# A GRU followed by a mixture of experts: the projections' bias added by VectorE as deferred work, zero copies and row deals moved to other steps

## The chip, the cores and the metric

The kernel runs on one core of a Trainium2 chip. Its time is the device time of one execution in microseconds (us). The kernel before was run three times: 1398.75, 1398.89 and 1401.8 us, median 1398.89 us. The engines are called PE (TensorE, matmuls; PEld is its weight load), DVE (VectorE), ACT (ScalarE), POOL (GpSimd) and SP (SyncE, which here only issues DMAs).

## What is computed

The reference runs a GRU over the time axis of `x` (8 sequences, 256 steps, 512 features) from the initial state `cond`, feeds its states to a mixture of experts (8 experts, the best 2 of each token, and a shared expert), and adds the result to `x`:

```python
def cell(h, x):
    gi = x @ W_ih + b_ih
    gh = h @ W_hh + b_hh
    i_r, i_z, i_n = jnp.split(gi, 3, axis=-1)
    h_r, h_z, h_n = jnp.split(gh, 3, axis=-1)
    r = jax.nn.sigmoid(i_r + h_r)
    z = jax.nn.sigmoid(i_z + h_z)
    n = jnp.tanh(i_n + r * h_n)
    h_new = (1.0 - z) * n + z * h
    return (h_new, h_new)
...
combine = jnp.sum(topk_w[..., None] * jax.nn.one_hot(topk_ids, E, dtype=x.dtype), axis=1)
gu = jnp.einsum('th,ehf->etf', x, w_gate_up)
eo = jnp.einsum('eti,eih->eth', _silu_and_mul(gu), w_down)
routed = jnp.einsum('te,eth->th', combine, eo)
shared = _silu_and_mul(x @ w_sh_gate_up) @ w_sh_down
return (routed + shared).reshape(orig_shape)
```

All arithmetic is float32. The 256 GRU steps are sequential; the input projections `x @ W_ih + b_ih`, the routing and the shared expert are not.

## The kernel before

**Blocks and steps.** The 256 steps are 16 blocks `k` of 16 steps `t`. `step(n)` issues the recurrent matmuls into the PSUM banks `ps_rn` and `ps_z` (L514), and then the chain that makes the next state: DVE transposes r, n and z (L527), ACT does the sigmoids and the tanh (L531, L537, L539) and opens the gates of the next step by copying the projections ("seeds") into PSUM (L486), DVE does the arithmetic (L534, L535, L542, L544) and writes the new state `hT` (L545). The next step's matmuls read `hT`. POOL copies one column of `hn` in every step (L543), so that POOL's later work starts only behind that point of the chain.

**Order.** The order on every engine is the order in which the program issues: `manual_schedule` leaves it as written. One engine's instruction that waits holds up all that were issued behind it on the same engine. SP issues nearly all DMAs and is tied to the steps only by what its DMAs wait for.

**What fills PE.** While the chain of step `n` runs, PE works on a queue of pieces (`matmul_piece`, `Piece`), 8 units of work in each step; a unit is four matmuls over 128 columns. The pieces are the input projections (`project(k, g)`, k the block, g = 0, 1, 2 for r, z, n; 4 pieces of 4 units each, L338) and, from block 2 on, the shared expert (`shared_unit`). They are issued behind `step(n)`, so on PE they stand between the matmuls of step `n` and those of step `n + 1`.

**A projection's end.** When the last piece of `project(k, g)` is issued, `end()` (for k > 0) has ACT copy the PSUM bank to the buffer `gi` (L432), POOL add the bias there (L433), and, after g = 1 and after g = 2, SP send `gi` to DRAM: `gid_rz` (512 KB, the r and z parts of `gi`, L441) and `gid_n` (256 KB, L443). There is one buffer `gi`; each g has its own third of it. Later, `load_seeds` (L475) reads the values back, four steps at a time.

**Deferred work.** `afterward(cost, work)` puts DVE work into one first-in, first-out list with a declared cost in us: the transpose of `x` for a projection (`turn_x_afterwards`, cost 1.1, L327), the product of the shared expert's halves (0.9, L769 and L770) and the final sum (0.66, L862). In each step, behind the chain, `catch_up(room)` takes work from the head of the list while the head's cost fits in what is left of `WINDOW = 1.1` (L350); DVE work that a step does directly (routing, `send_rows`) is taken off that room first. A piece that needs deferred work which has not been issued yet calls its `needed()`, which issues the list up to and including that item on the spot (for `x`: `turned_x.pop(k)()`, L412).

**Rows and zeros.** For the experts, every token's state is dealt into `dealt` in DRAM by an indirect DMA on POOL (`deal_rows`, L681), two per block. Before that, SP copies zeros there (`dealt<-blank`, 256 KB, L1029), eight copies in each block. A deal and a zero copy wait for the landing of the ones issued before them. The weights of the experts and of the shared expert are loaded by POOL's DMAs (`loads`, L166): one per step in blocks 0, 1 and 15, one in every odd step in the others, until the list is empty.

Of the kernel before, what the change touches and what calls it, by code (L numbers as in the profile page):

```python
# [13 lines left out]
ALU = mybir.AluOpType  # L14
# [11 lines left out]
def kernel(  # L26
# [52 lines left out]
    nc = tc.nc  # L79
    B, T, D = x.shape  # L80
    G3 = w_ih.shape[1]
    E = w_gate.shape[1]
# [9 lines left out]
    NM = NTOK // P  # L92
# [98 lines left out]
    def load_expert(e):  # L191
        load_up(e)
        load_down(e)
# [49 lines left out]
    def counting(name, n, base, step, channel):  # L243
# [31 lines left out]
    gi_later = const.tile([P, 4, 3, P], F32, name="gi")  # L275
# [3 lines left out]
        for i in (1, 0)  # L279
    ]  # L280
    gi_dram = [
        [
            dram.tile([4, B, TS, P], F32, name=f"gid_n_{i}"),
            dram.tile([4, B, TS, 2 * P], F32, name=f"gid_rz_{i}"),
        ]
        for i in range(1, NB)
    ]
# [13 lines left out]
    dealt = dram.tile([E * NM + 1, P, D], F32, name="dealt")  # L301
# [8 lines left out]
    blank = dram.tile([P, D], F32, name="blank")  # L310
# [23 lines left out]
    def multiply(ps, lhs, rhs, start, stop):  # L334


        for c in range(4):
            nc.tensor.matmul(  # L338
                ps[32 * c : 32 * c + 32],
                lhs(c),  # L340
                rhs,
                start=start,
                stop=stop,
                skip_group_check=True,
            )
# [29 lines left out]
    def matmul_piece(issue, end=None):  # L375
        return Piece(issue, end)

    def afterward(cost, work):
        item = [cost, work]
        afterwards.append(item)  # L380

        def needed():
            while item in afterwards:
                afterwards.popleft()[1]()

        return needed
# [3 lines left out]
    def bank_of(shape, name):  # L390
        if len(held) == 3:
            for needed in held[0]:
                needed()
        readers = []
        held.append(readers)
        return ps_mm.tile(shape, F32, tag="mm", name=name), readers
# [8 lines left out]
    def project(k, g):  # L405

        box = {}

        def issue(q, cols):
            if q == 0 and cols.start == 0:  # L410
                if k in turned_x:
                    turned_x.pop(k)()  # L412
                box["ps"], _ = bank_of([P, D], f"gip_{k}_{g}")
            multiply(
                box["ps"][:, cols],
                lambda c: xT_of[k][:, c, q, :],
                wih[:, q, g * D + cols.start : g * D + cols.stop],
                start=(q == 0 and cols.start == 0),
                stop=(q == NQ - 1 and cols.stop == D),
            )  # L420

        def by_group(t_):
            return t_.rearrange("p (q j i) -> p j q i", q=NQ, j=4)

        def end():
            gi = gi_later if k else gi_first
            to_gi = gi[:, :, g, :].rearrange("p j (q i) -> p j q i", q=NQ)
            bias_g = by_group(bias[:, g * D : (g + 1) * D])
            if k == 0:
                nc.vector.tensor_tensor(to_gi, by_group(box["ps"]), bias_g, ALU.add)  # L430
            else:
                nc.scalar.copy(to_gi, by_group(box["ps"]))  # L432
                nc.gpsimd.tensor_tensor(to_gi, to_gi, bias_g, ALU.add)  # L433
            if g > 0:
                projected.add((k, "rzn"[g]))
            if g > 0 and k == 0:
                send_first(g, 0)
            elif g > 0:
                to = gi_dram[k][g % 2].rearrange("j b t n -> (b t) j n")
                if g == 1:  # L440
                    nc.sync.dma_start(to.rearrange("p j (a n) -> p j a n", a=2), gi[:, :, 0:2, :])  # L441
                else:
                    nc.sync.dma_start(to, gi[:, :, 2, :])  # L443

        return [
            matmul_piece(lambda cols, q=q: issue(q, cols), end if q == NQ - 1 else None)
            for q in range(NQ)
        ]

    projected = set()  # L450

    def send_first(g, c):

        rows_ = slice(SC * B * c, SC * B * (c + 1))
        to = gi_first_dram[g % 2][c].rearrange("j t b n -> (t b) j n")
        if g == 1:
            nc.scalar.dma_start(to.rearrange("p j (a n) -> p j a n", a=2), gi_first[rows_, :, 0:2, :])
        else:
            nc.scalar.dma_start(to, gi_first[rows_, :, 2, :])
# [153 lines left out]
    def weigh_all(k):  # L613

        ch, w2 = chosen[k], weight_of[k]
        comb = said_0[:, :, 1]
        nc.vector.tensor_scalar(comb, ch[:, 0, :], w2[:, 0:1], None, ALU.mult)
        nc.vector.scalar_tensor_tensor(comb, ch[:, 1, :], w2[:, 1:2], comb, ALU.mult, ALU.add)
        nc.vector.tensor_scalar(
            said_0[:, :, 0], row_of.broadcast_to([P, E]), 0.0, None, ALU.add  # L620
        )
# [58 lines left out]
    def deal(tile_, at):  # L680
        nc.gpsimd.indirect_dma_start(  # L681
            out=dealt.rearrange("r p d -> (r p) d"),
            out_offset=bass.IndirectOffsetOnAxis(ap=at, axis=0),
            in_=tile_,
            in_offset=None,
        )

    def deal_rows(k, i):
        deal(rows_of[k], rows_at[k][:, i : i + 1])
# [116 lines left out]
    def load_again(k):  # L806

        again[k] = two.tile([P, D], F32, tag="again", name=f"again_{k}")
        nc.sync.dma_start(again[k], x[:, k * TS : (k + 1) * TS, :])
# [196 lines left out]
    for k in range(NB):  # L1006


        at = {}

        def when(t, cost, busy, work):
            at.setdefault(t, []).append((cost, busy, work))

        if k > 0:
            steps_ = (
                (0, choose, 1, 0), (1, sum_logits, 0.5, 0), (2, order_experts, 0, 1.2), (4, weigh, 0, 1.0),
                (5, count_places, 0.5, 0), (6, give_places, 0, 1.2), (8, send_rows, 0, 0.75), (10, read_rows, 0, 0),
            )
            late = int(k == 1)
            for t, f, cost, busy in steps_:  # L1020
                when(t + late, cost, busy, lambda f=f, k=k: f(k - 1))
            if k == 1:
                when(6, 0, 0.7, lambda k=k: weigh_all(k - 1))
            for i in range(2 if k > 1 else E):
                to_enter.append((k * TS + 8 + 2 * i, lambda k=k, i=i: enter(k - 1, i)))
            for i in range(2):
                when(12 + late + 2 * i, 0, 0, lambda k=k, i=i: deal_rows(k - 1, i))
        for e in range(E):
            when(2 + e, 0, 0, lambda k=k, e=e: nc.sync.dma_start(dealt[e * NM + k], blank))  # L1029
        if k > 1 and k % 2:  # L1030
            for b in (3, 2):
                when(6, 0, 0, lambda k=k, b=b: load_again(k - b))
        if k == 2:
            for e in range(3):
                load_expert(e)
            load_up(3)
        if k == NB - 1:
            load_down(3)
            for e in (E - 2, E - 1):
                load_expert(e)  # L1040
        quota = 33 * NQ if k < 2 else sum(p.left() for p in projections) / max(1, NB - 1 - k)
        while projections and quota > 0:
            quota -= projections[0].left()
            queue.append(projections.popleft())
        assert k == NB - 1 or len(projections) <= 13 * (NB - 2 - k), "the next block's are made"
        if k > 1:
            half = NSH * NF // 2
            for u in range(half):
                feed_shared(k // 2 - 1, half * (k % 2) + u)
        for t in range(TS):  # L1050
            n = k * TS + t
            step(n)
            if (n + 1) % SC == 0 and n + 1 < T and (n + 1) // SC + NS - 1 < T // SC:
                load_seeds((n + 1) // SC + NS - 1)
            room = WINDOW
            for cost, busy, work in at.get(t, ()):
                work()
                spent += cost
                room -= busy
            if to_enter and to_enter[0][0] == n:  # L1060
                to_enter.popleft()[1]()
            catch_up(room)
            if loads and (k < 2 or k == NB - 1 or t % 2):
                loads.popleft()()

            due += PER_STEP
            while queue and (queue[0].left() == 0 or due - spent >= queue[0].cost):
                spent += queue[0].run(due - spent)
                if queue[0].left() == 0:
                    queue.popleft()  # L1070
            if not queue:
                spent = due
# [4 lines left out]
    k = NB - 1  # L1077
# [77 lines left out]
```

## Time and profile before

| | |
|---|---|
| runs shown, median | 1398.89 us (1398.75 to 1401.8) |
| profiled execution's own time | 1401.84 us |
| its span, first to last instruction | 1400.0 us |
| mean granted PE clock | 0.996 |
| the 256 steps (first to last `hT`) | 37.28 to about 1148 us |
| PE busy, 33 to 1150 us | 1110.43 of 1117 us |
| DVE / ACT / POOL busy, 33 to 1150 us | 552.78 / 441.38 / 208.21 us |
| the bias on POOL (L433) | 45 instructions of 1274 ns |

A line of the timeline has its start, its duration, the engine, the source line, the operation, output and inputs by the program's names, and the count of instructions merged into it; in square brackets the idle time before it and what ended that. In a row of instruction groups, the part behind the first bar is busy time and mean ns of one, and behind the second bar the idle time before them. PE's matmuls are pipelined, and their ends are modelled.

The step is the distance between two starts of L545. Over the 255 distances it is 4.29 to 4.39 us, but for 21 of over 4.40 us, among them 5.68 us (step 14 to 15 of block 1), 5.24 us (step 0 to 1 of block 2), 5.04 and 4.83 us.

### The profile page before, as it was taken

Reading aid. Unit: us, or ns where it says so; the run is one execution under the profiler, and the core shown is the slowest. Engines: PE = TensorE matmul, PEld = TensorE weight load, DVE = VectorE, ACT = ScalarE, POOL = GpSimd, SP = SyncE. Lnnn points to the kernel's source line nnn. Section 1 sums busy time; section 2 is a strip of 40 time slices with the busy share of each in tenths; the row PEclk is TensorE's granted clock in tenths of the full one; section 3 lists DMA queues with packets and bytes.
Section 4 is the critical chain, followed back from the end, with each engine's and each line's share of the span. In section 5 each row is a group of like instructions: output and inputs, shape, how many; then the busy total and the mean of one; then the engine's idle time right before and its main releaser. Section 6 shows DMA issues by size and latency. Waiting matters only on the chain. (4 is left out here: it accounts for less than half of the span.)

```text
span 1400.0 us, 58934 instructions
## 1 busy us (share of the span) xinstructions
PE 1370.8 (98%) x24512; PEld 790.5 (56%) x24512; DVE 655.0 (47%) x2701; ACT 474.7 (34%) x2037; POOL 291.5 (21%) x564
## 2 busy tenths in 40 slices
PE   8999999999999999999999999999999999999996
PEld 3455657665656565656665666566655664444442
DVE  2445444545454544455544554555454543344442
ACT  0444343334343434343434343434343330111110
POOL 3333332121111111111111111111111122133332
PEclk9999999999999999999999999999999999999998
DMA  8544574332332232223222322232223454455553
GB/s 269 171 136 143 123 123 104 111 106 89 101 101 65 76 82 74 67 81 82 82 74 59 82 88 76 66 82 74 67 75 88 121 130 132 92 100 97 101 95 45
DMA packets 94082, 137.62 MB, mean 98 GB/s; under 512 B 17256, under 2 KB 67864, under 8 KB 91768
## 3 DMA queue, kind: packets, MB, share of 16 engines
q1 hardware_dynamic: 77192, 95.54, 24.9%
q0 software_dynamic: 15152, 37.38, 12.3%
q8 instruction: 194, 3.18, 1.0%
q10 hardware_dynamic: 1472, 0.93, 0.3%
q14 instruction: 72, 0.59, 0.1%
HBM read 94.55 MB, written 72.78 MB: 120 GB/s over the span
## 5 line engine op out<-in xcount | busy, mean ns | idle before, releaser
L514 PE MATMUL ps_rn<-we,hT 128*8 128x256 f32 x8192 | 492.1, 379 | 7.5 <-DVE hT L545 3.2
L514 PEld LDWEIGHTS ps_rn<-we,hT 128*8 128x8 f32 x8192 | 226.5, 89 | 254.1 <-ACT ps_z L486 52.0
L527 DVE STREAM_TRANSPOSE rT<-ps_rn 128x128 f32<-128x128 f32 x256 | 81.2, 317 | 436.8 <-PE ps_rn L514 436.8
L514 PE MATMUL ps_z<-we,hT 128*8 128x128 f32 x8192 | 274.3, 273 | 0.4 <-issue 0.4
L514 PEld LDWEIGHTS ps_z<-we,hT 128*8 128x8 f32 x8192 | 229.4, 90 | 50.0 <-issue 1.0
L531 ACT ACTIVATE rT<-rT 128x32 f32<-128x32 f32 x256 | 58.8, 230 | 527.8 <-DVE rT L527 517.8
L543 POOL COPY last_hn<-hn 128x1 f32<-128x1 f32 x256 | 47.3, 185 | 828.5 <-DVE hn L542 825.9
L824 PE MATMUL gu_s<-hc,wsu 128*32 128x256 f32 x3072 | 189.8, 379 | 0.0
L338 PE MATMUL gip<-we,xT 128*32 128x512 f32 (+2 forms) x1872 | 186.0, 520 | 1.7 <-DVE xT L220 1.7
L824 PEld LDWEIGHTS gu_s<-hc,wsu 128*32 128x32 f32 x3072 | 104.2, 110 | 56.5 <-issue 12.6
L778 PE MATMUL gu_t<-we,xrT 128*128 x280 | 131.4, 593 | 1.8 <-issue 1.8
L338 PE MATMUL po<-wsd,act_s 128*32 128x512 f32 (+2 forms) x1272 | 131.2, 509 | 0.2 <-DVE again L862 0.2
L338 PEld LDWEIGHTS gip<-we,xT 128*32 128x32 f32 x1872 | 61.0, 111 | 70.2 <-issue 59.9
L778 PEld LDWEIGHTS gu_t<-we,xrT 128*128 128x128 f32 x280 | 50.5, 190 | 52.9 <-issue 45.2
L527 DVE STREAM_TRANSPOSE zT<-ps_z 128x128 f32<-128x128 f32 x256 | 79.1, 309 | 0.3 <-PE ps_z L514 0.3
L548 ACT COPY hc<-hT 128x32 f32<-128x32 f32 x192 | 47.6, 248 | 91.2 <-DVE hT L545 88.9
L486 ACT COPY ps_rn<-seeds_n 128x128 f32<-128x128 f32 x256 | 69.1, 270 | 8.3 <-DMA seeds_n<-gid_n_first 0.2
L534 DVE TENSOR_TENSOR rT<-nT,rT 128x32 f32<-128x32 f32 x256 | 51.2, 200 | 42.8 <-ACT rT L531 42.2
L527 DVE STREAM_TRANSPOSE nT<-ps_rn 128x128 f32<-128x128 f32 x256 | 70.2, 274 | 0.0
L486 ACT COPY ps_rn<-seeds 128x128 f32<-128x128 f32 x256 | 69.0, 269 | 2.5 <-DMA seeds<-gid_rz_first 1.6
L542 DVE TENSOR_TENSOR hn<-hT,rT 128x32 f32<-128x32 f32 x256 | 49.3, 193 | 38.7 <-ACT rT L537 11.1
L433 POOL TENSOR_TENSOR gi<-gi,bias 128x512 f32<-128x512 f32 x45 | 57.3, 1274 | 46.0 <-ACT gi L432 45.4
(167 smaller groups left out, 1160.3 us busy)
## 6 DMA issues: line engine op xcount, KB each, us to landing
dealt<-blank SPq DMA_DIRECT2D x128, 256.0 KB
xr<-dealt SPq DMA_DIRECT2D x140, 64.0 KB
we<-in_L_ffn_w_gate_up_dram POOLq DMA_DIRECT2D x32, 256.0 KB, 6.8
gid_rz<-gi SPq DMA_DIRECT2D x15, 512.0 KB
seeds<-gid_rz SPq DMA_DIRECT2D x240, 32.0 KB
wsu<-_L_ffn_w_sh_gate_up_dram POOLq DMA_DIRECT2D x16, 256.0 KB, 5.6
rows<-hr SPq DMA_DIRECT2D x128, 32.0 KB
rb<-rows SPq DMA_DIRECT2D x16, 256.0 KB
```

Of the source, the lines that this page charges most:

```text
L338: nc.tensor.matmul(ps[32 * c : 32 * c + 32], lhs(c), rhs, start=start, stop=stop, skip_group_check=True,)
L433: nc.gpsimd.tensor_tensor(to_gi, to_gi, bias_g, ALU.add)
L486: nc.scalar.copy(gate_of[g], src)
L514: nc.tensor.matmul(banks[g][32 * j : 32 * j + B, 0 : n_ * P].rearrange("b (a k i) -> b a k i", a=n_, k=NQ), hT[:, q, 0:B], whh_v[:, q, j, ...
L527: nc.vector.transpose(gT.rearrange("p a b -> p (a b)"), gate_of[g])
L531: nc.scalar.activation(r, r, AF.Sigmoid)
L534: nc.vector.tensor_tensor(r, nT[:, :, 0:B], r, ALU.mult)
L542: nc.vector.tensor_tensor(hn, hT[:, :, 0:B], nn, ALU.subtract)
L543: nc.gpsimd.tensor_copy(last_hn, hn[:, 0, 0:1])
L548: nc.scalar.copy(hc_of_block(k).rearrange("p g q (c t) -> p q g c t", t=TS)[:, :, :, :, t], new.rearrange("p q (g c) -> p q g c", c=2),)
L778: nc.tensor.matmul(box["ps"], lhs(q), w_up(q), start=(q == 0), stop=(q == NQ - 1))
L824: nc.tensor.matmul(box["ps"][32 * g : 32 * g + 32, two_i, :], wsu[c][:, q, two_i, fs], hc_of[m][:, :, q, :], start=(two_i == 0 and q == 0) ...
```

## The change

The bias of the projections k > 0 is added by DVE. ACT's copy to `gi` stays where it was, in `end()`; the add becomes deferred work of cost 0.66, and the send to DRAM is issued behind the add. The first-in, first-out list is the one that holds the other deferred work. Before a third of `gi` is overwritten, its earlier add is issued if it was still in the list.

The deals of rows move from steps 12 and 14 (13 and 15 in block 1) to steps 13 and 15 in all blocks. The zero copies move from steps 2 to 9 to steps 0, 1, 2, 4, 6, 8, 10 and 12; in block 0 all are two steps later.

```diff
             if k == 0:
                 nc.vector.tensor_tensor(to_gi, by_group(box["ps"]), bias_g, ALU.add)
+                if g > 0:
+                    projected.add((k, "rzn"[g]))
+                    send_first(g, 0)
+                return
+            if g in biased:
+                biased.pop(g)()
+            nc.scalar.copy(to_gi, by_group(box["ps"]))
+            biased[g] = afterward(0.66, lambda: add_bias(to_gi, bias_g))
+
+        def add_bias(to_gi, bias_g):
+            nc.vector.tensor_tensor(to_gi, to_gi, bias_g, ALU.add)
+            if g == 0:
+                return
+            projected.add((k, "rzn"[g]))
+            to = gi_dram[k][g % 2].rearrange("j b t n -> (b t) j n")
+            if g == 1:
+                nc.sync.dma_start(to.rearrange("p j (a n) -> p j a n", a=2), gi_later[:, :, 0:2, :])
             else:
-                nc.scalar.copy(to_gi, by_group(box["ps"]))
-                nc.gpsimd.tensor_tensor(to_gi, to_gi, bias_g, ALU.add)
...
+                nc.sync.dma_start(to, gi_later[:, :, 2, :])
...
+    biased = {}
...
-                when(12 + late + 2 * i, 0, 0, lambda k=k, i=i: deal_rows(k - 1, i))
-        for e in range(E):
-            when(2 + e, 0, 0, lambda k=k, e=e: nc.sync.dma_start(dealt[e * NM + k], blank))
+                when(13 + 2 * i, 0, 0, lambda k=k, i=i: deal_rows(k - 1, i))
+        for e, t in enumerate((0, 1, 2, 4, 6, 8, 10, 12)):
+            when(t + 2 * (k == 0), 0, 0, lambda k=k, e=e: nc.sync.dma_start(dealt[e * NM + k], blank))
```

## The prediction, made before the result was known

> **What bounds the kernel now.** I read the page first: PE is busy for 1370.8 of 1400.0 us, and the groups give the price of what is moved (behind the bars: busy us and mean ns, then idle us before them).
>
> ```profile
> L534 DVE TENSOR_TENSOR rT<-nT,rT 128x32 f32<-128x32 f32 x256 | 51.2, 200 | 42.8 <-ACT rT L531 42.2 <-ACT ps_rn L486 0.5 <-issue 0.2
> ...
> L535 DVE TENSOR_TENSOR rT<-nT,rT 128x32 f32<-128x32 f32 x256 | 49.2, 192 | 8.8
> ...
> L433 POOL TENSOR_TENSOR gi<-gi,bias 128x512 f32<-128x512 f32 x45 | 57.3, 1274 | 46.0 <-ACT gi L432 45.4 <-issue 0.5
> ```
>
> Then the timeline of one step in the middle, PE's lines and DVE's:
>
> ```profile
> 608.24 1.91 PE L338 MATMUL gip<-we,xT 128*32 128x512 f32 x16
> 609.96 1.91 PE L514 MATMUL ps_rn<-we,hT 128*8 128x256 f32 x32
> ...
> 609.62 0.19 DVE L545 TENSOR_TENSOR hT<-rT,zT 128x32 f32<-128x32 f32 x1
> 609.73 1.14 DVE L327 STREAM_TRANSPOSE xT<-x 128x512 f32<-128x512 f32 x1
> 611.93 0.32 DVE L527 STREAM_TRANSPOSE rT<-ps_rn 128x128 f32<-128x128 f32 x1 [1.06 <-PE ps_rn L514]
> ```
>
> Call T the start of `hT` (609.62). The next recurrent matmuls start at T+0.34, the next chain at T+2.31 on DVE and at T+2.73 on ACT. PE's fill of 8 units ran from 608.24 to 609.96, 1.72 us or 0.215 us a unit: it ends just when `hT` is there. So chain and fill are level, and anything that holds either lengthens the step. DVE is free from T+0.19 to T+2.31, 2.1 us; ACT copies to `gi` at T+0.35 (609.97, 0.58 us) and is free until T+2.73 (L531 at 612.35). POOL's add follows that copy (610.64 to 611.92) and is over before the chain starts.
>
> **What the GpSimd add costs.** Next, the longest step, 5.68 us, in DVE's and POOL's timeline:
>
> ```profile
> 170.30 1.53 DVE L534 TENSOR_TENSOR rT<-nT,rT 128x32 f32<-128x32 f32 x1 [0.16 <-issue]
> ...
> 170.49 1.28 POOL L433 TENSOR_TENSOR gi<-gi,bias 128x512 f32<-128x512 f32 x1
> 171.70 0.19 POOL L543 COPY last_hn<-hn 128x1 f32<-128x1 f32 x1
> ```
>
> DVE's L534 lasts until POOL's add is over. L535 has the same shape and count and never meets the add; L534's surplus over it is 51.2 - 49.2 = 2.0 us, 1.3 of it here. The change removes these: **-2.0 us** (at least 1.3). The other 43 adds cost nothing on POOL: its work is off the chain, and L542 never waited for L543.
>
> **The add on DVE.** 45 adds at 0.69 us (L430, block 0's add of the same size, 685 ns), 31 us in the free 2.1 us behind the chain. I counted the deferred list by the rules of `catch_up`: no step gets more than 1.86 us of such work, which leaves 0.25. The ACT copy that an add needs ends over 3 us earlier. Cost on DVE: 0. Without the cover an add would cost 0.69 in its step. But the add queues in the same list as the transposes, and delays them. At all but two places the transpose is still a step or more ahead of the projection that reads it. The two are:
>
> **First: step 1 of block 0.** Before:
>
> ```profile
> 37.59 1.18 DVE L327 STREAM_TRANSPOSE xT<-x 128x512 f32<-128x512 f32 x1
> ...
> 40.22 1.91 PE L338 MATMUL gip<-we,xT 128*32 128x512 f32 x16
> ...
> 41.58 0.19 DVE L545 TENSOR_TENSOR hT<-rT,zT 128x32 f32<-128x32 f32 x1
> ...
> 41.94 1.92 PE L514 MATMUL ps_rn<-we,hT 128*8 128x256 f32 x32
> ```
>
> x_2 is transposed behind step 0, and step 1's fill (40.22) reads it. After the change the list before step 0 is: add (1,0) at 0.66, transpose of x_2 at 1.1, add (1,1) at 0.66. Step 0 takes the first (0.44 is left), step 1 the transpose, step 2 the second add. So the transpose stands on DVE behind `hT` of step 1, and PE's fill of step 1, which stands on PE before the matmuls of step 2, waits for it. With T = 41.58: transpose T+0.11 to T+1.26, PE on at T+1.42 (0.16 behind its release, as from L545's end to the matmuls), 8 units of 0.215 to T+3.14, where step 2's matmuls stood at T+0.34: **+2.8 us**, 2.6 to 3.0.
>
> **Second: step 9 of block 1.** The list holds add (5,0), x_6, add (5,1). Direct work of 1.0, 0.7 and 1.2 leaves steps 5, 6 and 7 too little room; step 8 does the add (before: the transpose of x_6). Step 9 has `send_rows`, 0.75, and nothing fits; but `project(6,0)` begins in its fill with 6 units and forces x_6 out on the spot, behind `hr`. From T of step 9: `hr` T+0.11 to T+0.82 (L668, 0.71), x_6 to T+2.0, PE T+2.16, 6 units to T+3.45 instead of T+0.34: **+3.1 us**, 2.8 to 3.3.
>
> **The send, and ACT's next copy into `gi`.** `gid_rz` leaves only after add (k,1), 1 to 3 steps later than before (the first at 31.94 before), and the copy (k+1,0) overwrites what it reads, so ACT waits for its landing, and the chain's sigmoid stands behind that copy. By the count, copy and send are at least 1.8 steps apart except twice. No wait shows a send's landing; the DMA windows around one that starts in a quiet stretch (825.86, with a zero copy behind) bound it:
>
> ```profile
> 827.00:827.50 0.50, 0.50 (x16) 0.25 (x12) 0.50 (x2) 0.25 (x1) 0.00 (x0) 1.00 0.98 352
> 827.50:828.00 0.50, 0.50 (x16) 0.23 (x8) 0.50 (x1) 0.00 (x0) 0.00 (x0) 1.00 0.97 338
> 828.00:828.50 0.50, 0.50 (x16) 0.29 (x12) 0.25 (x1) 0.00 (x0) 0.00 (x0) 1.00 1.14 268
> ```
>
> The last column is GB/s (131 in the half us before, none before 826.5). From 826.5 to 828.5 about 0.54 MB move, so 512 KB need 2.7 us from issue; 6.8 us is the median landing of POOL's 256 KB weight loads in traffic. I take 3.5, nearer the send's own row.
> - Block 0, step 2: add (1,1) ends at T+0.80, the send lands at T+4.3, the copy (2,0) of this step's fill ends at T+5.0, and the sigmoid due at T+2.73 waits: **+2.3 us**, 1.5 to 5.6.
> - Block 1, step 11: add (5,1) runs in step 10, the copy (6,0) is due in step 11. With T of step 9 and the 3.1 above, step 11's `hT` is at T+11.7, its sigmoid due at T+14.5. SP issues `hr`'s eight DMAs from T+0.9 (4.3 us), the eight loads of the next x (3.6 to 7.8), a zero copy (0.5), then the send: T+9.3 to T+13.5; landing and copy add 4.2: T+13.5 to T+17.7. Taking loads of 5.5 us: **+1.0 us**, 0 to 4.2 (a landing of 6.8 at that middling issue).
>
> The Trainium skill, "DMA: Bandwidth & Descriptors", section "Anatomy of one DMA — SWDGE (gpsimd) path", speaks against this change: a semaphore fires only after the target has confirmed the last byte, about 2.0 us fixed plus the bytes at 436 GB/s, so that reusing a source buffer waits for the whole write. That page's estimate is 3.2 us for 512 KB (its fit is for another issuing path), against 2.7 to the last bytes in the windows; by it the block-0 stall would be 2.0 and the sum 0.3 smaller.
>
> **Zero copies and deals.** SP is not held by steps: `load_seeds` gates it every fourth. Zero copies that went in bunches of up to four behind a `load_seeds` now go three, two, two, one. The deal at 13 waits for the zero copy of 12, which SP can issue by mid-step 11, and lands before 13; POOL may be a step late before L542 waits for L543. The next block's first zero copy waits for the deal of step 15, about 0.75 step into the block; behind it on SP stand sends, x loads and `load_seeds` of step 3, which can't start before step 2 anyway. In blocks 2 to 4 and 15 a deal (1.0) and a weight load (0.58) share a step of POOL: 1.6 of 4.3 us. Cost 0; the bounds are the long steps. Those over 4.40 hold 8.5 us over 4.32 together, 1.3 of them L534's. The rest come near zero copies at times (4.59 and 4.68 at bunches of four, but 4.39 at another). I take 0, with ends -2 and +2.
>
> **The sum.** -2.0 + 2.8 + 3.1 + 2.3 + 1.0 + 0 = **+7.2 us**, so 1409.0 for the profiled execution's 1401.84. That execution was 2.95 above the median of the runs, so the prediction is 1398.89 + 7.2 = **1406.1 us** (+0.5%). Likeliest case by its own bounds: 1401.8 to 1411.
>
> **Rivals.**
> - *Not slower: the moved zero copies clear the long steps.* Price: up to the 7.2 us of them that are not L534's, which makes 1398.9. For it: bunches at two long steps. Against: long steps with no zero copy issued in them (4.65 at step 7 of block 6). From 3.0 us cleared on it brings the result within 0.3%.
> - *The sends land late.* With 6.8 us, block 0 costs 5.6 and block 1 4.2: +13.7, 1412.6. For it: both fall in the stretch with weight loads in every step. Against: the quiet row.
> - *The change does what it says and no more:* some other work fills PE and ACT in these steps, and -2.0 is left, 1396.9. Against: the issue order on PE and ACT leaves nothing in between.
>
> **How the numbers follow.** The likeliest case 0.70, late sends 0.13, cleared long steps 0.13, no stall 0.04. A measurement here can tell about 0.3%, 4.2 us. Under 1394.7 needs no stall and cleared steps: 0.04. Within 0.3%: the rest of these two and the low tenth of the likeliest, 0.20. Slower: 0.76. The range goes from the low end of the likeliest to late sends: 1401.5 to 1412.
>
> **What would show it.** Right: step 1 to 2 of block 0 at about 7.1 us, with L327 behind `hT` of step 1 and PE's L338 waiting for it; step 2 to 3 at 6.6, with ACT's L432 waiting for the DMA of `gid_rz`; step 9 to 10 of block 1 at 7.4; 45 DVE adds of about 0.69 between L545 and L527; no L534 over 0.25 us. Wrong: those steps at 4.3, or many steps elsewhere changed by 0.1 or more.

## The result and the profile after

The changed kernel takes 1411.17 us (median of 6 runs, 1408.84 to 1417.8) against 1399.91 us (median of 6, 1398.75 to 1401.8), 11.3 us more by the medians; the measured ratio, which is not that of the two medians, is 1.0089 (95% interval 1.0074 to 1.0105). Measured twice more beside the kernel before, it was 1.0088 (1.0062 to 1.0115) and 1.0096 (1.0069 to 1.0124). The forecast was +7.2 us: the sign is right, the size too small. The medians of the two later measurements (1416.24 and 1416.67 us) lie above the forecast's range, that of the first just inside it. The kernel before was at 1402.22 and 1401.53 us beside those two, so by the medians they are +14.0 and +15.1 us.

The profiled execution took 1409.36 us (span 1407.6, mean granted PE clock 0.993; before 1401.84, 1400.0 and 0.996). From the first `hT` to the last it needs 1119.16 us, before 1111.03: +8.1 us. Line numbers have moved: `hT` is L552, DVE's transposes out of PSUM L534, the former L534 and L535 are L541 and L542, ACT's copy to `gi` L437, the bias add L441, the send `gid_rz` L447.

The groups first (busy us and mean ns, then idle us ahead of them and what ended it):

```profile
L541 DVE TENSOR_TENSOR rT<-nT,rT 128x32 f32<-128x32 f32 x256 | 49.3, 193 | 45.2 <-ACT rT L538 44.0 <-ACT ps_rn L493 0.9 <-issue 0.2
L542 DVE TENSOR_TENSOR rT<-nT,rT 128x32 f32<-128x32 f32 x256 | 49.1, 192 | 8.7
L441 DVE TENSOR_TENSOR gi<-gi,bias 128x512 f32<-128x512 f32 x45 | 30.8, 684 | 0.0
L437 ACT COPY gi<-gip 128x512 f32<-128x512 f32 x45 | 25.9, 579 | 23.9 <-DMA x<-in_x_dram 16.7 <-DMA gid_rz<-gi 5.3 <-PE gip L338 0.6
L338 PE MATMUL gip<-we,xT 128*32 128x512 f32 (+2 forms) x1872 | 186.6, 522 | 9.1 <-DVE xT L327 5.4 <-DMA we<-in_L_cond_W_ih_dram 2.2 <-DVE xT L220 1.6
```

The same copy and the same projection in the kernel before:

```profile
L432 ACT COPY gi<-gip 128x512 f32<-128x512 f32 x45 | 26.0, 580 | 19.1 <-DMA x<-in_x_dram 16.5 <-PE gip L338 2.6
L338 PE MATMUL gip<-we,xT 128*32 128x512 f32 (+2 forms) x1872 | 186.0, 520 | 1.7 <-DVE xT L220 1.7
```

The 45 adds now stand on DVE at 684 ns, and L541 is down to L542's level. Two waits are new: ACT's copy for the landing of `gid_rz` (5.3 us) and PE's projection for DVE's transpose (5.4 us). The timeline of steps 1 and 2 of block 0 (start us, duration us, engine, line, what; in brackets the idle time before):

```profile
41.60 0.19 DVE L552 TENSOR_TENSOR hT<-rT,zT 128x32 f32<-128x32 f32 x1
...
41.91 1.08 DVE L327 STREAM_TRANSPOSE xT<-x 128x512 f32<-128x512 f32 x1
...
43.14 3.41 PE L338 MATMUL gip<-we,xT 128*32 128x512 f32 x16 [2.71 <-DVE xT L327]
...
46.36 1.92 PE L521 MATMUL ps_rn<-we,hT 128*8 128x256 f32 x32
...
50.32 0.19 DVE L552 TENSOR_TENSOR hT<-rT,zT 128x32 f32<-128x32 f32 x1
50.43 0.69 DVE L441 TENSOR_TENSOR gi<-gi,bias 128x512 f32<-128x512 f32 x1
...
51.14 0.39 SPq L447 DMA_DIRECT2D gid_rz<-gi  x1
...
56.05 0.58 ACT L437 COPY gi<-gip 128x512 f32<-128x512 f32 x1 [5.26 <-DMA gid_rz<-gi]
56.54 0.23 ACT L538 ACTIVATE rT<-rT 128x32 f32<-128x32 f32 x1
...
58.10 0.19 DVE L552 TENSOR_TENSOR hT<-rT,zT 128x32 f32<-128x32 f32 x1
```

Both stalls are there as forecast, in their places: x_2 is transposed behind `hT` of step 1 and PE waits for it; the send leaves behind the add, and the copy (2,0) and with it the sigmoid (L538) wait until it has landed. What was not in the forecast is the duration 3.41: the 16 matmuls last 1.9 us in other steps. The windows of PE say why (PE busy us and count, then the granted clock, DMA share, GB/s):

```profile
40.00:42.00 2.00, 0.43 (x16) 1.00 0.26 68
42.00:44.00 2.00, 0.86 (x6) 0.69 0.68 250
44.00:46.00 2.00, 2.00 (x16) 0.50 0.11 35
46.00:48.00 2.00, 2.00 (x36) 0.95 0.41 131
```

Behind the idle 2.7 us, PE was granted half the clock for some 3.4 us (the windows lack 0.31, 0.50 and 0.05 of 2 us each, 1.7 us of clock in all; at half a clock lost that is 3.4 us). At step 9 of block 1 it is the same picture:

```profile
153.08 0.19 DVE L552 TENSOR_TENSOR hT<-rT,zT 128x32 f32<-128x32 f32 x1
153.19 0.70 DVE L675 STREAM_TRANSPOSE hr<-hc 128x512 f32<-128x512 f32 x1
...
153.82 1.03 DVE L327 STREAM_TRANSPOSE xT<-x 128x512 f32<-128x512 f32 x1
...
155.00 2.43 PE L338 MATMUL gip<-we,xT 128*32 128x512 f32 x16 [2.65 <-DVE xT L327]
...
162.22 0.19 DVE L552 TENSOR_TENSOR hT<-rT,zT 128x32 f32<-128x32 f32 x1
```

The clock was 0.60 from 155 to 157 us and 0.54 from 157 to 159. This table puts the kernels side by side (a step is the distance between two starts of `hT`, in us; "0.1" is step 1 to 2 of block 0, "1.11" step 11 to 12 of block 1; "all" is first to last `hT` against before's 1111.03). The rows below the first four are the experiments of the next section.

| kernel | 0.1 | 0.2 | 0.3 | 1.9 | 1.11 | 1.12 | 1.14 | all |
|---|---|---|---|---|---|---|---|---|
| before | 4.31 | 4.34 | 4.30 | 4.32 | 4.30 | 4.46 | 5.68 | 0 |
| changed | 8.72 | 7.78 | 4.29 | 9.14 | 4.31 | 4.32 | 4.35 | +8.1 |
| changed, second profile | 8.56 | 7.75 | 5.34 | 7.45 | 8.90 | 5.96 | 4.32 | +16.2 |
| changed, third profile | 8.78 | 8.12 | 5.49 | 7.45 | 9.23 | 5.72 | 4.34 | +15.1 |
| bias part alone | 8.91 | 8.04 | 6.55 | 7.45 | 9.19 | 5.72 | 4.34 | +17.4 |
| zeros and deals alone | 4.31 | 4.34 | 4.29 | 4.32 | 4.30 | 4.43 | 5.94 | -0.3 |
| adds behind the rest | 4.31 | 8.76 | 5.65 | 4.60 | 14.72 | 5.97 | 4.34 | +13.9 |
| second buffer | 7.22 | 4.38 | 4.28 | 8.87 | 4.30 | 4.32 | 5.84 | +7.8 |
| both cures | 4.31 | 4.39 | 4.29 | 4.32 | 4.30 | 5.70 | 6.68 | +3.4 |
| both cures, old zeros and deals | 4.32 | 4.38 | 4.29 | 4.32 | 4.30 | 5.18 | 5.85 | +0.9 |
| PE filled | 7.25 | 7.20 | 5.65 | 7.49 | 9.24 | 6.40 | 4.34 | +13.6 |
| weight load later | 7.21 | 7.94 | 4.29 | 9.14 | 6.39 | 4.29 | 4.35 | +9.8 |

### The profile page after: what moved, and what is told of

It reads as the page before. It is cut to its first block, busy times and chain, and to the rows that moved or that the text cites. A ratio compares the mean times of both kernels' runs of the same rounds, so it can differ in the third digit from the quotient of the medians.

```text
span 1407.6 us, 58885 instructions
## 1 busy us (share of the span) xinstructions
PE 1372.3 (97%) x24512; PEld 786.4 (56%) x24512; DVE 679.1 (48%) x2746; ACT 473.1 (34%) x2037; POOL 233.9 (17%) x519
## 5 line engine op out<-in xcount | busy, mean ns | idle before, releaser
L534 DVE STREAM_TRANSPOSE rT<-ps_rn 128x128 f32<-128x128 f32 x256 | 81.1, 317 | 420.5 <-PE ps_rn L521 420.5
L538 ACT ACTIVATE rT<-rT 128x32 f32<-128x32 f32 x256 | 58.5, 229 | 536.4 <-DVE rT L534 528.2
L831 PEld LDWEIGHTS gu_s<-hc,wsu 128*32 128x32 f32 x3072 | 101.4, 110 | 58.5 <-issue 12.6
L534 DVE STREAM_TRANSPOSE zT<-ps_z 128x128 f32<-128x128 f32 x256 | 79.0, 309 | 0.2 <-PE ps_z L521 0.2
L541 DVE TENSOR_TENSOR rT<-nT,rT 128x32 f32<-128x32 f32 x256 | 49.3, 193 | 45.2 <-ACT rT L538 44.0
L534 DVE STREAM_TRANSPOSE nT<-ps_rn 128x128 f32<-128x128 f32 x256 | 70.2, 274 | 0.0
L549 DVE TENSOR_TENSOR hn<-hT,rT 128x32 f32<-128x32 f32 x256 | 49.3, 192 | 37.8 <-ACT rT L544 11.4
L493 ACT COPY ps_z<-seeds 128x128 f32<-128x128 f32 x256 | 66.5, 260 | 0.0
```

What stands on the lines that cost most here:

```text
L493: nc.scalar.copy(gate_of[g], src)
L534: nc.vector.transpose(gT.rearrange("p a b -> p (a b)"), gate_of[g])
L538: nc.scalar.activation(r, r, AF.Sigmoid)
L541: nc.vector.tensor_tensor(r, nT[:, :, 0:B], r, ALU.mult)
L549: nc.vector.tensor_tensor(hn, hT[:, :, 0:B], nn, ALU.subtract)
L831: nc.tensor.matmul(box["ps"][32 * g : 32 * g + 32, two_i, :], wsu[c][:, q, two_i, fs], hc_of[m][:, :, q, :], start=(two_i == 0 and q == 0) ...
```

## The experiments

**The two halves of the change.** First the bias part with the zero copies and deals in their old steps:

```diff
-                when(13 + 2 * i, 0, 0, lambda k=k, i=i: deal_rows(k - 1, i))
-        for e, t in enumerate((0, 1, 2, 4, 6, 8, 10, 12)):
-            when(t + 2 * (k == 0), 0, 0, lambda k=k, e=e: nc.sync.dma_start(dealt[e * NM + k], blank))
+                when(12 + late + 2 * i, 0, 0, lambda k=k, i=i: deal_rows(k - 1, i))
+        for e in range(E):
+            when(2 + e, 0, 0, lambda k=k, e=e: nc.sync.dma_start(dealt[e * NM + k], blank))
```

> Only the bias part of the change; zero copies and deals in their old steps. Theory (the deferred list: two late transposes, and ACT waiting for a send): the same stalls as in the changed kernel, step 1 to 2 of block 0 at 8.2 to 8.8 us, step 2 to 3 at 7.3 to 8, step 9 to 10 of block 1 at 7.4 to 9.2, and the time 9 to 14 us above the kernel before. Rival (the moved zero copies or deals make the stalls): these steps near 4.3 and the time within 3 us of before.

Measured: 1417.77 us (1416.62 to 1418.86), ratio 1.0107 (1.0092 to 1.0123). The stalls are there, but it is 15.6 us above before by the medians, more than the 9 to 14 expected: step 1.11, which the expectation left out, is 9.19 us. Then the other half, these lines of the change alone in the kernel before:

> Only the zero copies and the deals are moved; POOL still adds the bias. If the zero copies are what shortened the other long steps of the changed kernel (about 3.3 us in its trace beside the GpSimd add's 1.8): 2 to 4 us faster than before, block 2 at about 70 us instead of 71.35. Rival (the long steps come and go by chance, or went with the GpSimd add): within 1.5 us of before. In both, L534 beside POOL's add in block 1 stays at up to 1.5 us.

Measured: 1401.98 us, ratio 1.0001 (0.9992 to 1.0010). The 2 to 4 us that were expected did not come. So the moved zero copies and deals by themselves are worth nothing that this measurement can tell, and the loss is the bias part's. The rival that the moved copies clear the long steps has fallen: in the zeros-alone kernel 2.0 is 5.58 us, 3.0 is 4.82 and 10.8 is 5.01, against 5.24, 4.83 and 5.04 before. The longest step there has the same cause as before, again in DVE's and POOL's timeline:

```profile
169.90 1.81 DVE L534 TENSOR_TENSOR rT<-nT,rT 128x32 f32<-128x32 f32 x1 [0.16 <-ACT rT L531]
170.37 1.29 POOL L433 TENSOR_TENSOR gi<-gi,bias 128x512 f32<-128x512 f32 x1
```

DVE's 0.19 us instruction is over only when POOL's add is.

**The late transposes: adds in a list of their own, behind the other deferred work.** If the adds push x_2 and x_6 back, the steps 0.1 and 1.9 are cured by this:

```diff
+        while adds and (room is None or adds[0][0] <= room):
+            cost, work = adds.popleft()
+            work()
+            if room is not None:
+                room -= cost
...
-            biased[g] = afterward(0.66, lambda: add_bias(to_gi, bias_g))
+            biased[g] = add_later(0.66, lambda: add_bias(to_gi, bias_g))
```

> The whole change, but the adds stand in a list of their own that gets what room the other deferred work leaves. Theory: the two transposes are back in time, steps 1 to 2 of block 0 and 9 to 10 of block 1 at 4.3, 9 us less than the changed kernel; the wait of ACT for the send stays in block 0 (step 2 to 3 at 7 to 8 us) and a second appears in block 1, step 11 to 12 (add (5,1) and copy (6,0) now fall in the same step), 2 to 4 us: in all 0 to 5 us above before. Rival (the adds on DVE themselves hold the chain): as slow as the changed kernel, 9 to 14 us above before.

Measured: 1416.91 us, ratio 1.0108 (1.0092 to 1.0124). Steps 0.1 and 1.9 are 4.31 and 4.60 us: the order in the list made those two stalls. But the time did not fall to the 0 to 5 us above before that were expected; it is 14.7 us above by the medians, since a later add is a later send. SP's and ACT's timeline of block 1:

```profile
158.12 5.48 SPq L499 DMA_DIRECT2D seeds<-gid_rz  x4
...
165.53 0.67 SPq L702 DMA_DIRECT2D rb<-rows  x1
166.30 0.40 SPq L464 DMA_DIRECT2D gid_rz<-gi  x1
...
171.51 0.59 ACT L454 COPY gi<-gip 128x512 f32<-128x512 f32 x1 [12.19 <-DMA gid_rz<-gi]
```

The send now stands on SP behind the seeds and the read of the rows; ACT waits 12.2 us for it, and 1.11 is 14.7 us.

**The send waits: a second `gi` buffer.** Blocks 2, 4 and 6 use the buffer that block 0 used, so that no copy overwrites what a send still reads:

```diff
-            gi = gi_later if k else gi_first
+            gi = gi_first if k in (0, 2, 4, 6) else gi_later
...
```

> The whole change, with a second buffer for gi in blocks 0, 2, 4 and 6, so that ACT's copy overwrites nothing that a send still reads. Theory: step 2 to 3 of block 0 at 4.3 instead of 7.8, the two late transposes unchanged (8.7 and 9.1, or 7.1 and 7.4 where PE's clock is not lowered): 5 to 9 us above before. Rival (that step is long for another reason, the landing of seeds or a PE wait): it stays at 7 to 8 us.

Measured: 1412.35 us, ratio 1.0073 (1.0058 to 1.0088). Step 0.2 is 4.38 us, and this is ACT's and SP's timeline there:

```profile
49.33 0.59 ACT L437 COPY we<-gip 128x512 f32<-128x512 f32 x1 [0.17 <-PE gip L338]
49.50 0.39 SPq L447 DMA_DIRECT2D gid_rz<-gi  x1
```

The copy (2,0), here to a buffer that the trace calls `we`, goes ahead of the send of the other. So the wait was for the reuse of the buffer. Step 1.11 is free of it too, which this profile alone does not show, as the first profile of the changed kernel has no wait there either; with both cures, below, the copy in 1.11 goes 6.6 us and more ahead of the send. The time is 10.2 us above before by the medians, where 5 to 9 were expected: the two late transposes are left, one of them with the halved clock (1.9 at 8.87).

**The clock: PE filled while it waits.** Eleven more matmuls, whose result nobody reads, ahead of `project(2, 0)` and `project(6, 0)`: added work, in the time in which PE would idle.

```diff
                 if k in turned_x:
                     turned_x.pop(k)()
+                if g == 0 and k in (2, 6):
+                    for _ in range(11):
+                        nc.tensor.matmul(banks["x"][:, 0:P], ident, ident, start=True, stop=True)
```

> The changed kernel, with 11 matmuls of 128x128 (some 2.4 us, into a PSUM bank that nothing reads at that time) issued on PE ahead of the first pieces of project(2,0) and project(6,0), where PE waits for the late transposes. Theory (after 2.6 us of waiting PE's granted clock is halved for about 3.4 us, which the waits' price left out): the steps 1 to 2 of block 0 and 9 to 10 of block 1 take 7.1 to 7.5 us with the clock at 1.0 there, against 8.7 and 9.1 in the changed kernel's trace, and the time is 1.5 to 4 us below the changed kernel's. Rival (the surplus is DVE's or the transposes'): they stay at 8.7 to 9.1 or grow by the matmuls.

PE's timeline (the 11 matmuls stand there as 22 records) and its windows in step 0.1:

```profile
38.99 2.72 PE L415 MATMUL ps_x<-ident 128*128 128x128 f32 x22
41.79 1.92 PE L338 MATMUL gip<-we,xT 128*32 128x512 f32 x16
```

```profile
42.00:44.00 2.00, 2.00 (x28) 1.00 0.61 197
44.00:46.00 2.00, 2.00 (x57) 1.00 0.45 131
```

The clock stays at 1.00, the projection takes 1.92 us although it waits for the same transpose, and 0.1 and 1.9 are 7.25 and 7.49 us: the forecast's 7.1 and 7.4. Later in the same execution stands a wait that was not filled, that for the send of block 0, and behind it the clock is halved, and the recurrent matmuls take 3.26 us instead of 1.92:

```profile
55.01 3.26 PE L524 MATMUL ps_rn<-we,hT 128*8 128x256 f32 x32 [2.66 <-DVE hT L555]
```

```profile
54.00:56.00 2.00, 0.99 (x12) 0.59 0.21 57
56.00:58.00 2.00, 2.00 (x28) 0.55 1.06 314
```

By itself the fill does not prove that idle time halves the clock, because unfilled waits too are followed by full clock in some executions: 0.1 is 7.22 us with the second buffer and 7.21 with the later load. Over all the profiles with these two waits unfilled, 0.1 and 1.9 are 1.3 to 1.7 us longer in the seven cases with a halved clock than in the five without, so two steps at full clock could come by chance about once in six. What backs it beyond this is that in the four profiles in which PE never idles for 2 us between the first step and the last (before, zeros and deals alone, both cures with either zero copies) the granted clock is 1.00 in every 100 us from 40 to 1140 us.

The whole kernel took 1414.47 us (1413.54 to 1416.58), ratio 1.0089 (1.0069 to 1.0108). The unaltered kernel beside it, shown next, has 1416.24 us and 1.0088, so the 1.5 to 4 us that were expected cannot be told from nothing. The send waits were left in, and one of them was at its worst in the profiled execution (1.11 at 9.24). The case for the clock rests on the steps, not on the time.

**The unaltered kernel again.**

> The changed kernel unaltered, on the same chip as the three others. Theory: the same waits in the same steps (1 to 2, 2 to 3 of block 0, 9 to 10 of block 1), 7 to 14 us above before, with a halved clock behind some of these waits and not behind the same ones as in the first trace.

Measured: 1416.24 us (1412.31 to 1419.88), ratio 1.0088 (1.0062 to 1.0115). The wait that the first profile did not show is here, in ACT's, SP's and PE's timeline of step 1.11:

```profile
165.97 0.53 SPq L447 DMA_DIRECT2D gid_rz<-gi  x1
...
174.57 0.59 ACT L437 COPY gi<-gip 128x512 f32<-128x512 f32 x1 [6.37 <-DMA gid_rz<-gi]
...
176.95 3.58 PE L521 MATMUL ps_rn<-we,hT 128*8 128x256 f32 x32 [4.38 <-DVE hT L552]
```

From issue to copy the send took 8.6 us, where in the first profile it had landed within 3.8 us (issued at 163.04, copy at 166.88 without a wait); PE was idle for 4.4 us, and the recurrent matmuls behind it, 1.92 us elsewhere, took 3.58 us. So a profile of one execution is not enough here: the same program has this wait in some executions and not in others.

**Why that send lands late.** In three profiled executions the last weight load of the blocks 0 and 1 (256 KB, by POOL) was issued ahead of the send by 0.3 to 1.8 us, and the sends took 8.0, 8.6 and 9.5 us; in the first profile the send came first, by 0.9 us. So the load was moved out of its way, with the unaltered kernel as control on the same chip:

```diff
-            if loads and (k < 2 or k == NB - 1 or t % 2):
+            if loads and n not in (26, 27) and (k < 2 or k == NB - 1 or t % 2):
```

> The changed kernel with one edit: no weight load is issued in steps 10 and 11 of block 1; the one that stood there (256 KB, by POOL) goes to step 12. Theory: the send (5,1) of block 1 lands late because that load was issued ahead of it: in the executions where the load came first by 0.3 to 1.8 us the send took 8.0 to 9.5 us, and in the one where the send came first by 0.9 us it had landed 3.8 us after its issue. Then step 11 of block 1 is at 4.3 to 4.5 us here, ACT's copy of gi there waits under 0.5 us, the two late transposes and the send wait of block 0 stay (steps 1 and 2 of block 0 and step 9 of block 1 at 7.2 to 9.1), and the time is some 4 to 6 us under that of the unaltered changed kernel where that one has its wait. Rival: the send is late by SP's own traffic ahead of it (x loads, zero copy, seeds); then step 11 is at 8.9 us as in the last execution and the times are equal.

> The changed kernel unaltered, as the control for the load moved later on the same chip: 1409 to 1417 us. Where its weight load of step 10 of block 1 (POOL) is issued ahead of the send (5,1), step 11 of block 1 is at about 8.9 us; where behind it, at 4.3.

Measured: 1414.16 us (1410.39 to 1419.51) with the load later, ratio 1.0096 (1.0063 to 1.0129); 1416.67 us (1411.32 to 1418.16) unaltered, ratio 1.0096 (1.0069 to 1.0124). The control's load came 1.2 us ahead of the send, the send took 8.6 us, and 1.11 was 9.23 us. With the load out of the way it is 6.39 us, neither the 4.3 of the theory nor the 8.9 of the rival, and the time is 2.5 us under the control's by the medians where 4 to 6 were expected, with equal ratios:

```profile
162.66 0.53 SPq L447 DMA_DIRECT2D gid_rz<-gi  x1
...
170.31 0.59 ACT L437 COPY gi<-gip 128x512 f32<-128x512 f32 x1 [3.86 <-DMA gid_rz<-gi]
```

```profile
164.00:166.00 2.00, 2.00 (x51) 1.00 0.77 258
166.00:168.00 2.00, 2.00 (x44) 1.00 0.64 53
168.00:170.00 2.00, 2.00 (x55) 1.00 0.62 37
```

The send still took 7.6 us. In the windows (the last two columns are the DMA engines' busy share and GB/s) most bytes move before 166 us; then the engines are busy for 0.6 of the time while next to nothing moves. The load ahead of the send is therefore not the whole cause; what holds the DMA engines in those microseconds stays open.

**Both cures together**, the adds behind the rest and the second buffer, first with the new zero copies and deals, then with the old:

> The whole change with both remedies: the adds in a list of their own behind the other deferred work, and the second buffer for gi in blocks 0, 2, 4 and 6. Theory: all four long waits are gone (every step of blocks 0 and 1 under 5 us), the GpSimd add's 2 us stays saved: 1 to 4 us faster than before (ratio 0.997 to 0.9995). Rival (31 us of adds on DVE cost something of their own, or late sends hold another place): 2 us or more above before.

> As e5_last_two, with zero copies and deals in the steps of the kernel before. If the moved zero copies are worth anything by themselves, this is slower than e5_last_two by 1 us or more; theory, after e2_zeros_only: within 1.5 us of it, since they mattered only to when the sends landed.

Measured: 1404.71 us, ratio 1.0016 (1.0007 to 1.0025), and 1403.11 us, ratio 1.0012 (0.9999 to 1.0024). All four stalls are gone (0.1, 0.2, 1.9, 1.11 at 4.3 to 4.4 us), and the loss is down to 0.1 to 0.2%: the late transposes, the waits for sends and the clock behind them are most of what the change costs. Which zero copies are used cannot be told apart here (the intervals overlap). Neither kernel beats the one before, although 1 to 4 us less had been expected of the first: the 2 us that DVE's L541 gains are eaten by other long steps, with the old zero copies 1.12 (5.18), 1.14 (5.85), 2.5 (4.80, before 4.29) and 12.2 (4.96, before 4.33).

Most such long steps do not come and go with the execution. Over 4.40 us the kernel before has 24 steps (not 21, as counted ahead of the prediction), and 20 of them stand in the same places with the zeros and deals alone, 18 of these within 0.03 us. From block 2 on, 14 steps are long, only one of them (15.9) among these 24, in all three profiles of the changed kernel, the bias part alone, the filled one and the later load, each within 0.01 us of itself (6.1 at 4.57, 9.13 at 4.68, 10.6 at 4.72; before 4.29, 4.32 and 4.35). So their places go with the program. Outside 0.1 to 0.4, 1.9, 1.11 and 1.12 the steps over 4.40 hold 8.3 us over 4.32 in the kernel before, 4.2, 6.4 and 4.5 in the three profiles of the changed one, but 10.7 and 8.9 with both cures. What makes a step long is not shown.

1.14 looks like this in PE's, POOL's and DVE's timeline:

```profile
167.45 2.08 PE L538 MATMUL ps_rn<-we,hT 128*8 128x256 f32 x32
...
169.17 1.23 PE L538 MATMUL ps_z<-we,hT 128*8 128x128 f32 x22
169.34 0.97 POOL L682 DMA_INDIRECT listed<-said,pl  x1 [0.16 <-issue]
170.72 0.49 PE L538 MATMUL ps_z<-we,hT 128*8 128x128 f32 x9 [0.32 <-issue]
170.82 0.32 DVE L551 STREAM_TRANSPOSE rT<-ps_rn 128x128 f32<-128x128 f32 x1 [3.06 <-PE ps_rn L538]
```

PE stops in the middle of the recurrent matmuls for nothing that the profile shows ("issue"), for 0.32 us, and DVE takes up `ps_rn` only 1.3 us after the last of its matmuls by the modelled ends. I have no cause for it, and no run that tells one apart.

## Why the prediction was right and wrong, step by step

- **-2.0 us, DVE's L534 behind POOL's add: right.** The group goes from 51.2 to 49.3 us, -1.9; no instruction of it is over 195 ns.
- **The add on DVE, 0: right.** 45 adds of 683 to 693 ns, idle 0.0 ahead of them, and no chain starts behind one of them.
- **+2.8 us, x_2 in step 1 of block 0: mechanism right, size short.** At full clock the step is 7.21 to 7.25 us, +2.9 (three kernels above); the transpose starts 0.31 us behind `hT`, not 0.11, as in step 0 before. In the three profiles of the changed kernel it is 8.56 to 8.78, +4.3 to +4.5. The step of the prediction that failed is "8 units of 0.215": PE was priced at full clock behind an idle time that this same working had made 2.7 us long; in the first profile the 8 units took 3.41 us in place of 1.92.
- **+3.1 us, x_6 in step 9 of block 1: the same.** 7.45 us (+3.1) in two of the three profiles, 9.14 (+4.8) in the first, where the clock was halved.
- **+2.3 us, the send of block 0: right place, short.** The second term that was mis-sized: the landing was taken as 3.5 us; it took 4.9 (51.14 to 56.05), so the step cost 3.4 to 3.8. In the two later profiles the halved clock behind it adds 1.0 and 1.2 us in the next step, and 0.6 and 0.5 in the one after that. The estimate of 3.2 us by the Trainium skill, "DMA: Bandwidth & Descriptors", section "Anatomy of one DMA — SWDGE (gpsimd) path", which the prediction weighed, was further off; that page has the semaphore fire only after the last byte is confirmed, and ACT's wait of 5.26 us for the send's completion agrees.
- **+1.0 us, the send of block 1: wrong as a size.** A middling value was taken between 0 and 4.2. What the executions have is one or the other end: 0 in the first profile, +4.6 and +4.9 in the two later ones, and 1.3 to 1.5 more in the step behind for the clock. The landing is 3.8 us or less, or 8.6.
- **0 for zero copies and deals: right,** by the kernel that has them alone. What does change elsewhere is another thing: the long steps 2.0 and 3.0 (5.24 and 4.83) are 4.3 in all three profiles of the changed kernel and with the bias part alone, but stay with the zeros alone. So they are gone where DVE adds the bias, about 1.4 us that the prediction did not count; whether POOL's add lengthened them is not shown. More generally, outside the stalls and the steps behind them 38 steps of the first profile differ by 0.1 us or more from before (7 with the zeros alone). "Many steps elsewhere changed by 0.1 or more" was one of the prediction's own signs of being wrong: it had no term for it.
- **The sum.** Over the six steps from 0.1 to 1.12 in the table and step 0.4, each against 4.32 us, the three profiles have +12.6, +18.7 and +19.3 us where the prediction had 9.2; over the rest -4.5, -2.5 and -4.3 where it had -2.0, most of it in the long steps counted above. The first profile's total, +8.1, is near the forecast's 7.2 by luck: two late transposes with a halved clock (1.6 and 1.7 us over their terms) and the longer landing (1.1 over) are cancelled by the missing wait in 1.11 (1.0 under) and by the rest (2.5 under).
- **The rivals.** "Sends land late" (1412.6) came nearest: in block 1 its 6.8 us landing is what five of the six profiled executions with the one buffer and the one list exceed. But in block 0 the landing was 4.3 to 5.3 us in them, and the case left out the clock. "No stall" and "cleared long steps" have fallen: long steps do hold 2 to 4 us less in the changed kernel, but the moved zero copies are not the reason.

The term that was missing altogether is the clock. In the places where PE idled for about 2.7 us ahead of the fill (0.1 and 1.9, in the changed kernel's three profiles, the bias part alone, the second buffer and the later load), the next 3.4 us ran at half clock in seven of twelve cases, for 1.3 to 1.7 us; behind the idle time of step 1.11, 4.4 to 4.7 us long, in all four cases seen; behind that of step 0.2, 2.7 to 3.6 us long, in four of the six profiles with the one buffer and the one list, where with the bias part alone it lasted longer (0.50 from 59 to 63 us, and 0.3 is 6.55 us). The Trainium skill, "TensorE: Matmul & The Clock Gate", Part 1, has the clock set by an activity window of 3413 ns that runs freely and puts PE to half speed after an idle window. That the runs differ and that half speed mostly lasts about 3.4 us agrees with it. But these gaps of 2.65 to 2.71 us are shorter than such a window, and the page's advice ("Why this matters for your kernels") to keep idle gaps under some 3 us is too generous for these rows, in which they were enough in seven of twelve cases. With up to 1.7 us behind each of the four stalls, the case of late sends would have stood at 1412.6 + 6.8 = 1419.4 us, and the range would have reached there. That idle time is what halves the clock is argued from these counts, the filled steps and the kernels without such waits; no run separates it from everything else that differs between executions.

## What to carry to other kernels

Work put into a first-in, first-out list costs its effect on what stands behind it in the list, not its own duration: 31 us of adds fit into free DVE time, and yet the steps as a whole take 8 to 16 us longer, through two late transposes, two late sends and the clock behind them. When a stall leaves PE idle for 2.6 us or more (the shortest seen here), price what follows at half clock for the next 3.4 us, as a chance and not as a certainty. A gain of 2 us in a kernel like this can also be undone by long steps whose places change with the program. A buffer that a DMA reads is busy from the DMA's place in its queue until it has landed; with a landing that varies from under 4 to over 9 us, move the reuse away from it (the second buffer took the waits out) rather than reckon with a mean.

## What the runs showed of the hardware

- The same idle gap is followed by full clock in one execution and by half clock in another: in the later-load kernel PE waited 2.71 us in step 0.1, just as in the first profile, and its fill took 1.92 instead of 3.41 us.

```profile
43.92 1.92 PE L338 MATMUL gip<-we,xT 128*32 128x512 f32 x16 [2.71 <-DVE xT L327]
```

- A send of 512 KB from SBUF to DRAM took from 3.8 us or less to 9.5 us from issue to the copy that waited for it, in the same place of nearly the same program.
- The changed kernel's runs spread over 11 us (1408.84 to 1419.88 over the three measurements), the kernel before's over about 7 (1398.75 to 1405.82). The two chances above, clock and landing, come and go with the execution and are of that size; that they make the whole spread is argued, not shown.
